# Mirrored odd blocks and one more unit of the products with B on GpSimd, in a stack of state-space scans

## The chip, the cores and the metric

The kernel runs on one core of a Trainium2 chip. The metric is the time of one execution in microseconds, as the device reports it; a kernel's time is the median of its runs. The engines are named as in the profile: PE (TensorE), ACT (ScalarE), DVE (VectorE), POOL (GpSimd) and SP (SyncE, which here issues the DMAs).

## The reference

Eight images of 48 x 48 positions and 96 channels pass through four residual layers. Layers 0 and 3 are 2-D selective scans (called "2-D" below, `ss2d` in the code), layer 2 scans every line of the image separately ("lines"), layer 1 is a spectral layer with no scan and is not touched. The core of a scan, cut to what matters:

```
xs = stack([x0, x1, x0[..., ::-1], x1[..., ::-1]])   # rows, columns, both reversed: 4 directions k
dts, Bs, Cs = split(x_dbl)                           # projections of xs: 16 states N each for B and C
delta = softplus(dts + bias)
def step(h, inp):                                    # over the positions of the sequence
    dA = exp(dl[..., None] * A)
    h  = h * dA + (dl * u)[..., None] * Bv[:, :, None, :]
    y  = einsum('bkdn,bkn->bkd', h, Cv)              # sum over the 16 states
    return h, y
```

Each direction has 192 channels with 16 states. In the 2-D layers one sequence covers the whole image (2304 positions), so a state goes on from row to row; in the lines layer every line of 48 positions starts from zero.

## The kernel before

**Blocks and turns.** A sequence of 2304 positions is cut into five blocks (`BLKS`, L25): four full ones of 10 rows (480 positions) and a short one of 8 rows (384), number 4. `scans` (from L172) walks over 8 images x 4 directions x 5 blocks = 160 blocks a layer, backwards through the blocks in the reverse directions. A block has 8 half-turns, or slots (`NG = 8`), each of a group of states and half of the channels. A slot holds three units; a unit is 128 partitions (32 channels x 4 states) by the positions of the block. Two slots make a turn, so a block has four turns q = 0 to 3, and a turn has six units in one `dbu` buffer, of which there are four.

**A turn, in the order of the code (L350 to L395).** ScalarE makes the decays `exp(dt * A)` in PSUM (`make_da`, L255), two units at a time, in two buffers. VectorE and GpSimd multiply `dt*u` by B (`make_dbu`, L235). In even slots VectorE makes all three units; in odd slots `ON_POOL` (L40) says how many of the three GpSimd makes. VectorE reads B from a copy in PSUM that ScalarE makes (`copy_b`, L216), GpSimd from the `bc` tile in SBUF. VectorE then scans two units in one instruction (`scan`, L263), in place in `dbu`, backwards for the reverse directions. GpSimd multiplies the states by C in place, three units at a time (`make_hc`, L276), and TensorE sums over the states (`reduce`, L296 and L298). In turn t the code works on the first products of turn t+1, and the products with C of the second half of turn t-1.

**Carried states.** One scan instruction runs over two units laid end to end. In the 2-D layers a unit therefore has one column more than positions (`columns`, L67: m = n + 1). Its decay is exp of a huge negative number, zero (`FAR`, written by the memset in `make_du`, L427), so the scan forgets what came before, and its addend is the state that the previous block left. The state travels in three steps. After a scan GpSimd copies the last column of three units into a small tile `carry` (`keep`, L270). One block later ScalarE copies six carried states (or `zero`, for the first block of a direction) into the extra columns of the new `dbu` (`bring`, L243), just before the decays of the next turn. The scan of that turn picks them up. In the lines layer no state is carried; the first position of each line has zero decay instead.

**Work beside the turns.** Two blocks ahead, `stage1` makes the inputs of a block step by step, one step at each half-turn, called from `aside`: projections on TensorE, softplus on ScalarE (L629, with its table loads), `dt*u` on GpSimd (`make_du`, L422), stores to DRAM (`store_dd`, L410), from where SP loads them broadcast over states (`load_dd`, L192, `load_bc`, L204). Convolutions, norms and the output of other images are strewn in the same way. Every engine takes its instructions in the order of the code.

Of the kernel before, what the change touches and what calls it, by code (L numbers as in the profile page):

```python
# [9 lines left out]
F32 = mybir.dt.float32  # L10
# [15 lines left out]
BMAX = 480  # L26
WMAX = BMAX + 1
NG = 8
# [10 lines left out]
CH = 96  # L39
ON_POOL = {1: 1, 3: 2, 5: 1, 7: 2}  # L40

# [17 lines left out]
class Block:  # L59


    def __init__(self, job, k, blk, first, last, rev):
        self.job, self.k, self.blk, self.first, self.last, self.rev = job, k, blk, first, last, rev
        self.r0, self.nr = BLKS[blk]
        self.n = self.nr * SEG

    def columns(self, restart):  # L67

        self.m = self.n + (0 if restart else 1)
        self.col = None if restart else self.n if self.rev else 0  # L70
        at = 0 if restart or self.rev else 1
        self.at = slice(at, at + self.n)


@with_exitstack
def vss_stack_kernel(ctx: ExitStack, tc: tile.TileContext, i: dict, out: bass.AP):
# [89 lines left out]
    def scans(dirs, order, restart, a, pools, ps, stage1, opening, done, side, tail):  # L166
# [6 lines left out]


        blocks = [Block(job, k, blk, n == 0, n == len(BLKS) - 1, dirs[k][1])
                  for job in range(nb) for k in order
# [4 lines left out]
        nt = len(turns)  # L181
        carry = pools["carry"].tile([P, 24], F32, tag="carry", name="carry")
        zero = pools["carry"].tile([P, 6], F32, tag="zero", name="zero")
        nc.gpsimd.memset(zero, 0.0)
        dbus, das, bps, bcs, ys = {}, {}, {}, {}, {}
# [9 lines left out]
        def load_bc(t):  # L195

            b, slot = blocks[t // NG], t % NG
            sg = ORDER[slot][1]
            other = t - slot + NG - 1 - slot
            n = min(free, key=lambda n: free[n])  # L200
            free[n] = other
            r = pools["bc"].tile([P, 2 * BMAX], F32, tag=f"bc{n}", name=f"bc{n}")
            rows4 = b.bcd[8 * sg:8 * sg + 8, :].rearrange("(s w) n -> s (w n)", w=2)
            nc.sync.dma_start(r[:, :2 * b.n], rows4.unsqueeze(0).to_broadcast([32, 4, 2 * b.n]))  # L204
            bcs[t] = bcs[other] = r[:, :2 * b.n].rearrange("p (w n) -> p w n", w=2)

        def copy_b(t):

            if t >= NG * len(blocks):
                return  # L210
            b, slot = blocks[t // NG], t % NG
            if slot == NG // 2:
                bps[t] = bps[t - 1]
                return
            bps[t] = ps("b", 1)
            nc.scalar.copy(bps[t][:, :b.n], bcs[t][:, 0, :b.n])  # L216

# [3 lines left out]
        def make_dbu(t, engine):  # L221

            if t >= NG * len(blocks):
                return
            b, slot = blocks[t // NG], t % NG
            if t // 2 not in dbus:
                dbus[t // 2] = pools["dbu"].tile([P, 6 * WMAX], F32, tag="dbu", name="dbu")
            cut = 3 - ON_POOL.get(slot, 0)
            lo, hi = (0, cut) if engine is nc.vector else (cut, 3)
            if lo == hi:  # L230
                return
            o = units(dbus[t // 2], b, 3 * (slot % 2) + lo, 3 * (slot % 2) + hi)[:, :, b.at]
            du = b.got[ORDER[slot][0]][:, lo:hi, 1, b.at]
            by = bps[t][:, :b.n] if engine is nc.vector else bcs[t][:, 0, :b.n]
            engine.tensor_mul(o, du, by.unsqueeze(1).to_broadcast([P, hi - lo, b.n]))  # L235

        def bring(t):

            if t >= nt or restart:
                return  # L240
            b, q = turns[t]
            o = units(dbus[t], b, 0, 6)[:, :, b.col]
            nc.scalar.copy(o, zero if b.first else carry[:, 6 * q:6 * q + 6])  # L243

# [12 lines left out]
        def scan(t, pair):  # L257
            b, q = turns[t]
            da = das.pop((t, pair))[:, :2 * b.m]
            db = dbus[t][:, 2 * pair * b.m:(2 * pair + 2) * b.m]  # L260
            if b.rev:
                da, db = da[:, ::-1], db[:, ::-1]
            nc.vector.tensor_tensor_scan(db, da, db, 0.0, ALU.mult, ALU.add)  # L263

        def keep(t, sub):
            b, q = turns[t]
            if b.last or restart:
                return
            last = b.at.start if b.rev else b.at.stop - 1
            nc.gpsimd.tensor_copy(carry[:, 6 * q + 3 * sub:6 * q + 3 * sub + 3], units(dbus[t], b, 3 * sub, 3 * sub + 3)[:, :, last])  # L270

        def make_hc(t, sub):
            b, q = turns[t]
            n = b.n
            h = units(dbus[t], b, 3 * sub, 3 * sub + 3)[:, :, b.at]
            nc.gpsimd.tensor_mul(h, h, bcs.pop(2 * t + sub)[:, 1, :n].unsqueeze(1).to_broadcast([P, 3, n]))  # L276

# [40 lines left out]
        for t in range(-2 * NG, 0):  # L318
            run(t)
        for half in range(2):  # L320
            load_dd(blocks[0], half)
# [6 lines left out]
        copy_b(2)  # L328
        bring(0)
        make_da(0, 0)  # L330
# [17 lines left out]
        for t, (b, q) in enumerate(turns):  # L348
# [7 lines left out]
            if t > 0:  # L356
                keep(t - 1, 1)
                make_hc(t - 1, 1)
# [11 lines left out]
            aside(at)  # L370
            bring(t + 1)
            keep(t, 0)
            make_hc(t, 0)
# [5 lines left out]
            if q == NG // 2 - 1 and b.k == order[-1] and b.last:  # L379
                for _ in beside:  # L380
                    while tail:
                        tail.pop(0)()
        keep(nt - 1, 1)
        make_hc(nt - 1, 1)
# [7 lines left out]
    def scan_pools(stack):  # L392
        def pool(name, bufs, **kw):
            return stack.enter_context(tc.tile_pool(name=name, bufs=bufs, **kw))
        ps = pool("ps", 1, space=PSUM)  # L395

        def psum(tag, bufs, n=512):
            return ps.tile([P, n], F32, tag=tag, name=f"ps_{tag}", bufs=bufs)

        pools = {"dd": pool("dd", 3), "bc": pool("bc", 1), "dbu": pool("dbu", 4),  # L400
                 "carry": pool("carry", 1), "dds": pool("dds", 1), "bcl": pool("bcl", 1),
                 "dr": pool("dr", 4, space=DRAM)}
        return pools, psum
# [13 lines left out]
    def make_du(b, half, u):  # L417
# [4 lines left out]
        nc.gpsimd.tensor_mul(rows(du, n), rows(dt, n), u)  # L422
        if b.col is None:
            at = SEG - 1 if b.rev else 0
            nc.gpsimd.memset(rows(dt, n)[:, :, at:at + 1], FAR)
        else:
            nc.gpsimd.memset(b.dds[:, half, :2 * b.m].rearrange("p (t m) -> p t m", t=2)[:, :, b.col:b.col + 1], FAR)  # L427


    def ss2d(l, xin, xout, b0=0):  # L430
# [163 lines left out]
        def stage1(b):  # L594
            n = b.n
            u = seq(us[b.job], dirs[b.k][0])[:, :, b.r0:b.r0 + b.nr, :]
            got = {}
# [42 lines left out]
        def so_far(b, half):  # L640
            if b.job not in yss:
                yss[b.job] = big.tile([DH, 2, L], F32, tag="big", name="ysum")
            return seq(yss[b.job][:, half], dirs[b.k][0])[:, b.r0:b.r0 + b.nr, :]

        def opening(b, half):

            if b.k == 0:
                return dskip[:, half, :], us[b.job][:, half, b.r0 * W:b.r0 * W + b.n]
            return wc["ident"], so_far(b, half)
# [480 lines left out]
```

## Time and profile before

| | |
|---|---|
| median of 3 runs | 19436.81 us (19431.89 to 19439.07) |
| the profiled execution | 19445.46 us, its span 19443.7 us |
| first to last scan, layer 0 / lines / layer 3 | 5807 / 6112 / 5810 us |
| busy: DVE, POOL, PE, ACT | 87%, 82%, 78%, 73% of the span |

A line of a group names the line of the kernel, the engine, the operation, what it writes and reads, and the shapes; then, after the count, its busy time in us, the mean ns of one instruction, and the idle time of the engine just before these instructions with what ended it. A line of a stretch gives the stretch, its length, and then the busy time (and number of instructions) of PE, PE's weight loads, DVE, ACT and POOL, and last the granted clock, the DMA engines' share and GB/s. A line of the order of time has a start, a length, and in brackets the idle time before it. A line of waits has who waited for whom, us in total, times, and the longest.

### The profile page before, as it was taken

Reading aid. Unit: us, or ns where it says so; the run is one execution under the profiler, and the core shown is the slowest. Engines: PE = TensorE matmul, PEld = TensorE weight load, DVE = VectorE, ACT = ScalarE, POOL = GpSimd, SP = SyncE. Lnnn points to the kernel's source line nnn. Section 1 sums busy time; section 2 is a strip of 40 time slices with the busy share of each in tenths; the row PEclk is TensorE's granted clock in tenths of the full one; section 3 lists DMA queues with packets and bytes.
Section 4 is the critical chain, followed back from the end, with each engine's and each line's share of the span. In section 5 each row is a group of like instructions: output and inputs, shape, how many; then the busy total and the mean of one; then the engine's idle time right before and its main releaser. Section 6 shows DMA issues by size and latency. Waiting matters only on the chain.

```text
span 19443.7 us, 172969 instructions
## 1 busy us (share of the span) xinstructions
PE 15206.3 (78%) x53500; PEld 4384.0 (23%) x53500; DVE 16830.2 (87%) x11289; ACT 14190.2 (73%) x22262; POOL 16019.2 (82%) x9825
## 2 busy tenths in 40 slices
PE   6777777777777897888888988887777777777776
PEld 1211211211114562222222222222121121121121
DVE  7999999999993228999999999997999999999998
ACT  6777877877872227788788787786778778778776
POOL 6999999999991007888888888886999999999998
PEclk6776776776767777888888878878677677677675
DMA  4444444444443324444434444443444444444444
GB/s 135 162 159 162 160 159 162 159 161 161 156 165 60 49 43 147 145 142 151 149 141 147 147 143 146 147 145 119 158 162 159 160 162 160 157 162 161 157 162 138
DMA packets 768487, 2829.45 MB, mean 146 GB/s; under 512 B 235724, under 2 KB 298668, under 8 KB 640926
## 3 DMA queue, kind: packets, MB, share of 16 engines
q1 hardware_dynamic: 767558, 2818.38, 44.1%
q8 instruction: 422, 6.91, 0.1%
q14 instruction: 507, 4.15, 0.1%
HBM read 2371.42 MB, written 446.69 MB: 145 GB/s over the span
## 4 chain that ended last, share of the span: by engine, by line
DVE 32%; PE 19%; POOL 16%; ACT 15%; issue 13%; DMA 5%; SPq 0%; POOLq 0%; DVEq 0%; ACTq 0%
DVE dbu L263 20%; POOL dbu L276 12%; DVE dbu L235 11%; ACT ps_da L255 4%; PE ps_s L740 3%; ACT L255 3%; PE ps_y L296 3%; DMA dd<-dd 2%; PE ps_h L970 2%; POOL dds L422 2%; PE ps_s L611 2%; PE ps_y L983 2%; PE ps_s L812 1%; POOL dbu L235 1%; PE ps_side L482 1%
## 5 line engine op out<-in xcount | busy, mean ns | idle before, releaser
L263 DVE TENSOR_TENSOR_SCAN dbu<-ps_da,dbu 128x962 f32<-128x962 f32 (+3 forms) x5760 | 11853.3, 2070 | 927.4 <-ACT ps_da L255 925.1
L276 POOL TENSOR_TENSOR dbu<-dbu,bc 128x1440 f32<-128x1440 f32 (+1 forms) x3840 | 11433.5, 2984 | 1051.2 <-DVE dbu L263 837.5
L255 ACT ACTIVATE ps_da<-dd,w_l_a 128x481 f32<-128x481 f32 (+3 forms) x11520 | 7414.9, 648 | 2754.7 <-DVE dbu L263 2548.7
L296 PE MATMUL ps_y<-dbu,w_red 128*32 128x480 f32 (+1 forms) x23040 | 4947.0, 747 | 2996.0 <-POOL dbu L276 2991.6
L298 PE MATMUL ps_y<-dbu,w_red 128*32 128x480 f32 (+1 forms) x7680 | 4906.1, 747 | 0.0
L235 DVE TENSOR_TENSOR dbu<-dd,ps_b 128x1440 f32<-128x1440 f32 (+5 forms) x3840 | 4641.3, 1209 | 261.3 <-ACT ps_b L216 217.7
L235 POOL TENSOR_TENSOR dbu<-dd,bc 128x480 f32<-128x480 f32 (+3 forms) x1920 | 3023.4, 1575 | 58.8 <-DMA bc<-bcd 35.5
L296 PEld LDWEIGHTS ps_y<-dbu,w_red 128*32 128x32 f32 x23040 | 743.6, 125 | 6938.7 <-POOL dbu L276 5185.4
L216 ACT COPY ps_b<-bc 128x480 f32<-128x480 f32 (+1 forms) x3360 | 1798.8, 535 | 298.9 <-DVE dbu L235 270.1
L740 PE MATMUL ps_s<-xpad,w_l_cw 128*128 128x480 f32 (+1 forms) x2560 | 1760.7, 840 | 2.3 <-ACT xpad L124 1.6
L482 PE MATMUL ps_side<-xpad,w_l_cw 128*128 128x480 f32 (+1 forms) x2880 | 1652.6, 703 | 4.5 <-ACT xpad L124 4.5
L255 ACT ACT_TABLE_LOAD x986 | 1265.0, 1283 | 17.5
L113 POOL MEMSET w_l_cw<- 128x1760 f32 (+1 forms) x3 | 5.8, 1941 | 1346.3 <-DVE x L950 1340.9
L422 POOL TENSOR_TENSOR dds<-dds,u 96x480 f32<-96x480 f32 (+1 forms) x640 | 791.9, 1237 | 202.9 <-ACT dds L629 202.9
L601 PE MATMUL ps_s<-bcl,dtw 6*96 6x480 f32 (+1 forms) x1280 | 880.6, 777 | 90.7 <-ACT dds L605 80.9
L611 PE MATMUL ps_s<-u,w_l_xp 96*38 96x480 f32 (+1 forms) x1280 | 931.7, 867 | 2.8 <-ACT dds L605 1.5
L270 POOL COPY carry<-dbu 128x3 f32<-128x3 f32 x2048 | 382.5, 187 | 635.0 <-DVE dbu L263 628.5
L292 PE MATMUL ps_y<-ysum,w_ident 96*96 96x480 f32 (+1 forms) x960 | 747.5, 868 | 114.1 <-ACT ysum L652 112.6
L482 PEld LDWEIGHTS ps_side<-xpad,w_l_cw 128*128 128x128 f32 x2880 | 581.1, 227 | 1130.4 <-issue 940.9
L740 PEld LDWEIGHTS ps_s<-xpad,w_l_cw 128*128 128x128 f32 x2560 | 531.8, 213 | 1096.4 <-issue 961.9
L298 PEld LDWEIGHTS ps_y<-dbu,w_red 128*32 128x32 f32 x7680 | 683.1, 125 | 0.0
L768 PE MATMUL ps_s<-bcl,dtw 6*96 6x480 f32 (+1 forms) x640 | 424.1, 799 | 181.7 <-ACT bcl L762 181.7
(146 smaller groups left out, 12660.7 us busy)
## 6 DMA issues: line engine op xcount, KB each, us to landing
dd<-dd SPq DMA_DIRECT2D x512, 1443.0 KB
bc<-bcd SPq DMA_DIRECT2D x1536, 480.0 KB
dd<-dd SPq DMA_DIRECT2D x256, 1440.0 KB
dd<-dds SPq DMA_DIRECT2D x512, 360.8 KB
dd<-dd SPq DMA_DIRECT2D x128, 1155.0 KB
bc<-bcd SPq DMA_DIRECT2D x384, 384.0 KB
dd<-dds SPq DMA_DIRECT2D x256, 360.0 KB
dd<-dd SPq DMA_DIRECT2D x64, 1152.0 KB
```

Source lines behind the costliest of these rows:

```text
L216: nc.scalar.copy(bps[t][:, :b.n], bcs[t][:, 0, :b.n])
L235: engine.tensor_mul(o, du, by.unsqueeze(1).to_broadcast([P, hi - lo, b.n]))
L255: nc.scalar.activation(da[:, at:at + b.m], b.got[half][:, u % 3, 0, :], AF.Exp, scale=a[:, b.k, ci:ci + 1])
L263: nc.vector.tensor_tensor_scan(db, da, db, 0.0, ALU.mult, ALU.add)
L276: nc.gpsimd.tensor_mul(h, h, bcs.pop(2 * t + sub)[:, 1, :n].unsqueeze(1).to_broadcast([P, 3, n]))
L296: nc.tensor.matmul(y[32 * g:32 * g + 32, :n], lhsT=wc["red"][:, :32], rhs=hc[:, g, b.at], start=False, stop=(slot == 3))
L298: nc.tensor.matmul(y[DH:, :n], lhsT=wc["red"][:, 32:], rhs=hc[:, 2, b.at], start=(slot == 0), stop=(slot == 3))
L422: nc.gpsimd.tensor_mul(rows(du, n), rows(dt, n), u)
L482: nc.tensor.matmul(pu[:, :n], lhsT=flat[:, at:at + P], rhs=xpad[:, r0 + dy:r0 + dy + nr, dx:dx + W], start=(tap == 0), stop=(tap == 8))
L601: nc.tensor.matmul(got["p"][:DH, :n], lhsT=dtw[2 * NS:, b.k, half, :], rhs=b.bcl[2 * NS:, :n], start=True, stop=True)
L611: nc.tensor.matmul(got["p"][:NBC, :n], lhsT=w[f"{l}_xp"][:, b.k, half, :], rhs=u[:, half], start=(half == 0), stop=(half == 1))
L740: nc.tensor.matmul(got["u", half][:, :n], lhsT=flat[:, at:at + P], rhs=shifted(off), start=(tap == 0), stop=(tap == 3))
```

## The change

**Mirrored blocks.** In the 2-D layers, blocks 1 and 3 are kept in reverse order of positions: `view` reads the inputs u, and reads and writes the sums y, backwards in both dimensions, and the scan of a mirrored block runs the other way through its buffer. A unit now has two columns more than positions (m = n + 2): one at the end where the scan begins (`came`), with decay zero as before, and one where it ends (`goes`), with decay 1 (dt = 0) and addend 0 (dt*u = 0), so that the scan leaves the final state there. The next block in the sequence scans in the opposite sense, and its `came` is the same column of the same buffer; the four buffers, `rooms`, are now allotted once, one to each turn of a block. So `keep`, `bring`, `carry` and `zero` are gone. `begin` has work only where a direction starts (a memset) and where the block's length changes between the short block and a full one (a copy of five states a partition on GpSimd).

**Where things lie.** The products with B take the column `goes` along, so that it becomes zero. The B and C rows in `bc` now start at element 1 of the tile instead of 0, in all three scan layers; `bc` tiles too are allotted once. `make_du` writes the end columns of both halves in two memsets, with the first half.

**The split.** In slot 5, in all three scan layers, GpSimd makes two of the three units instead of one.

```diff
-WMAX = BMAX + 1
+WMAX = BMAX + 2
-ON_POOL = {1: 1, 3: 2, 5: 1, 7: 2}
+ON_POOL = {1: 1, 3: 2, 5: 2, 7: 2}
...
     def columns(self, restart):
-        self.m = self.n + (0 if restart else 1)
-        self.col = None if restart else self.n if self.rev else 0
-        at = 0 if restart or self.rev else 1
-        self.at = slice(at, at + self.n)
+        self.mirrored = not restart and self.blk % 2 == 1
+        self.back = self.rev != self.mirrored
+        if restart:
+            self.m = self.n
+            self.at = self.by = slice(0, self.n)
+            return
+        self.m = self.n + 2
+        self.at = slice(1, self.n + 1)
+        self.came, self.goes = (self.m - 1, 0) if self.back else (0, self.m - 1)
+        self.by = slice(0, self.n + 1) if self.back else slice(1, self.n + 2)
+    def view(self, t, col):
+        v = seq(t, col)
+        if len(v.shape) == 3:
+            v = v[:, self.r0:self.r0 + self.nr, :]
+            return v[:, ::-1, ::-1] if self.mirrored else v
...
-            r = pools["bc"].tile([P, 2 * BMAX], F32, tag=f"bc{n}", name=f"bc{n}")
+            r = bufs[n]
-            nc.sync.dma_start(r[:, :2 * b.n], rows4.unsqueeze(0).to_broadcast([32, 4, 2 * b.n]))
-            bcs[t] = bcs[other] = r[:, :2 * b.n].rearrange("p (w n) -> p w n", w=2)
+            nc.sync.dma_start(r[:, 1:1 + 2 * b.n], rows4.unsqueeze(0).to_broadcast([32, 4, 2 * b.n]))
+            lead = b.at.start
+            bcs[t] = bcs[other] = r[:, 1 - lead:1 - lead + b.m], r[:, 1 + b.n:1 + 2 * b.n]
...
-        def bring(t):
+        def begin(t):
             if t >= nt or restart:
                 return
             b, q = turns[t]
-            o = units(dbus[t], b, 0, 6)[:, :, b.col]
-            nc.scalar.copy(o, zero if b.first else carry[:, 6 * q:6 * q + 6])
+            o = units(rooms[q], b, 0, 6)[:, :, b.came]
+            if b.first:
+                nc.gpsimd.memset(o, 0.0)
+            elif blocks[t // (NG // 2) - 1].m != b.m:
+                c = blocks[t // (NG // 2) - 1]
+                nc.gpsimd.tensor_copy(o[:, 1:], units(rooms[q], c, 1, 6)[:, :, c.goes])
...
-        def keep(t, sub):
-            b, q = turns[t]
-            if b.last or restart:
-                return
-            last = b.at.start if b.rev else b.at.stop - 1
-            nc.gpsimd.tensor_copy(carry[:, 6 * q + 3 * sub:6 * q + 3 * sub + 3], units(dbus[t], b, 3 * sub, 3 * sub + 3)[:, :, last])
...
             if t > 0:
-                keep(t - 1, 1)
                 make_hc(t - 1, 1)
...
-            bring(t + 1)
-            keep(t, 0)
+            begin(t + 2)
             make_hc(t, 0)
             make_da(t + 1, 0)
```

## The prediction

> **What bounds the kernel now.** I read the busy line and the groups of the page first, then one long stretch of each kind of layer, then groups by shape, then the order of time around the vector engine's stalls.
>
> ```profile
> PE 15206.3 (78%) x53500; PEld 4384.0 (23%) x53500; DVE 16830.2 (87%) x11289; ACT 14190.2 (73%) x22262; POOL 16019.2 (82%) x9825
> ...
> L263 DVE TENSOR_TENSOR_SCAN dbu<-ps_da,dbu 128x962 f32<-128x962 f32 (+3 forms) x5760 | 11853.3, 2070 | 927.4 <-ACT ps_da L255 925.1
> L276 POOL TENSOR_TENSOR dbu<-dbu,bc 128x1440 f32<-128x1440 f32 (+1 forms) x3840 | 11433.5, 2984 | 1051.2 <-DVE dbu L263 837.5
> ```
>
> See who waits for whom: idle time before the scans is ended by ScalarE's exponentials, 925.1 of 927.4 us, and never by GpSimd; GpSimd waits for the scans. By stretch (span, then PE, PEld, DVE, ACT, POOL), the first line 2-D (ss2d), the second lines:
>
> ```profile
> 2000.00:3000.00 1000.00, 761.78 (x2660) 197.05 (x2660) 934.04 (x591) 785.14 (x1272) 918.81 (x623) 0.74 0.48 161
> 9000.00:10000.00 1000.00, 834.86 (x2632) 222.82 (x2630) 923.63 (x629) 807.89 (x1172) 874.12 (x420) 0.81 0.41 144
> ```
>
> VectorE is the bound in both (934, 924), with GpSimd close behind (919, 874). From the scans taken in order, a 2-D block takes 36.3 us on average (5807 us over 160; a full one 37.4) and a lines block 38.2. Splitting the idle time before scans by its place in a full block: 2-D has 0.58 us before the first scan of a block (positive in 82% of full blocks) and 0.94 before the second; lines has 1.06 before the first scan of turn 0 and 0.67 before the first of turn 1. Turns 2 and 3 run without stalls in both.
>
> **Price of GpSimd's products.** Groups by shape, for a forward stretch of a 2-D layer (2310 to 2660 us), a reverse one (2680 to 3030), and lines (9000 to 9700):
>
> ```profile
> L276 POOL TENSOR_TENSOR dbu<-dbu,bc 128x1440 f32<-128x1440 f32 x60 | 179.2, 2986 | 4.8
> ...
> L235 POOL TENSOR_TENSOR dbu<-dd,bc 128x960 f32<-128x960 f32 x15 | 30.9, 2058 | 0.0
> ...
> L235 POOL TENSOR_TENSOR dbu<-dd,bc 128x480 f32<-128x480 f32 x14 | 14.5, 1036 | 0.0
> ```
> ```profile
> L276 POOL TENSOR_TENSOR dbu<-dbu,bc 128x1440 f32<-128x1440 f32 x67 | 205.4, 3068 | 10.5 <-DVE dbu L263 6.3
> ...
> L235 POOL TENSOR_TENSOR dbu<-dd,bc 128x480 f32<-128x480 f32 x18 | 21.4, 1189 | 0.0
> ```
> ```profile
> L276 POOL TENSOR_TENSOR dbu<-dbu,bc 128x1440 f32<-128x1440 f32 x115 | 371.3, 3244 | 59.7 <-DVE dbu L263 57.9 <-DMA bc<-bcd 1.7
> ...
> L235 POOL TENSOR_TENSOR dbu<-dd,bc 128x960 f32<-128x960 f32 x29 | 64.8, 2235 | 0.0
> L235 POOL TENSOR_TENSOR dbu<-dd,bc 128x480 f32<-128x480 f32 x28 | 34.0, 1213 | 3.1 <-DMA dd<-dd 3.1
> ```
>
> One shape has several prices. Lines gives a slow unit: 2235 - 1213 = 1.02 us; forward gives a fast one, 1036 - (1213 - 1022) = 0.85. Held against the columns where operands start, every row fits one rule: a unit is fast when its first operand starts 2 or 3 elements past a multiple of 4 relative to the second operand, slow at 0 or 1. Lines: all at 0, three slow. Forward half-turns: 1, 2, 3 (one slow, 2.90) and 0, 1, 2 (two slow, 3.07), mean 2.986; reverse: always two slow, 3.07. In all of these the second operand starts at a multiple of 4, so whether the difference or the first operand alone counts is not shown.
>
> **The change, part by part.**
>
> *The moved unit* (slot 5, every layer). VectorE's rows for two units and one are 1.129 and 0.629 in full blocks, 0.928 and 0.528 in short ones: -0.50 and -0.40 us a block. Against that, two more columns a scan: (2150 - 1750)/(962 - 770) = 2.08 ns an element, 12 scans, 0.050 us; one more column in 17 product units, 0.018. 2-D: 256 x 0.432 + 64 x 0.332 = 132 us. Lines (no wider rows): 128 x 0.50 + 32 x 0.40 = 77.
>
> A rule speaks against it. The Trainium skill, Perfetto Trace Analysis, section Optimizing Scalar/DVE Operations, says that moving work between VectorE and GpSimd may not help since they share an SBUF read port. By the rule the 132 would be 0 and the wider rows a loss of 21. The rows say otherwise: VectorE's one-unit product takes 628, 629 and 628 ns in the three stretches, scans 2149 to 2150, beside a busy GpSimd. I take the rows.
>
> *GpSimd's load.* The Trainium skill, GPSIMD Engine Reference, section Elementwise: about 2.6 cycles an element for two inputs, 1.04 us a unit at 1.2 GHz; the trace has 1.02 or 0.85. In 2-D the new columns (width 482, data from 1, C from 481) give two and one slow units alternately, mean 2.99 (before 3.03 over both directions), and make all products with B fast: 1.04 for one unit, 1.88 for two. Per full block: 8 x 2.99 + 1.04 + 3 x 1.88 = 30.6, against 8 x 3.03 + 2 x 1.12 + 2 x 2.06 = 30.6. The unit is free there. By the skill's price it is +1.0. The 2048 carry copies go (start to start 0.27 each, some 1.7 us a block); begin puts back 4 small instructions in two blocks of five, 0.4. The net is -1.3 us a 2-D block, or -0.3 by the skill. In lines B and C now start one past a multiple of 4 while data stay at 0: if the difference counts, all units are fast and GpSimd falls by some 4 us a block; if only the first operand counts, it rises by 1.0, from 874 to some 900 in 1000, still under VectorE.
>
> *ScalarE's carry copies go*, 1280 x 0.19 us, with their waits. In the order of time around the end of a block (ScalarE, then VectorE):
>
> ```profile
> 3120.62 1.28 ACT L629 ACT_TABLE_LOAD   x1
> 3121.91 0.85 ACT L629 ACTIVATE dds<-dds 96x768 f32<-96x768 f32 x1
> 3122.66 0.19 ACT L243 COPY dbu<-carry 128x6 f32<-128x6 f32 x1
> 3122.87 1.28 ACT L255 ACT_TABLE_LOAD   x1
> 3124.16 1.36 ACT L255 ACTIVATE ps_da<-dd,w_l_a 128x481 f32<-128x481 f32 x2
> ```
> ```profile
> 3125.56 2.16 DVE L263 TENSOR_TENSOR_SCAN dbu<-ps_da,dbu 128x962 f32<-128x962 f32 x1 [0.30 <-ACT ps_da L255]
> ```
>
> The copy stands between softplus and the exponentials that this scan waits for. Where that stall exists, 0.20 us of it go: the mean of min(stall, 0.20) is 0.16 in full and 0.15 in short blocks, 256 x 0.16 + 64 x 0.15 = 51 us. Next late is the exponential itself.
>
> *An earlier GpSimd in 2-D.* ScalarE's copy of the projections (L616) waits for a matmul queued behind reductions that wait for GpSimd, which sometimes stalls the second scan of turn 1 (0.11 us a full block, 1.38 a short one, 116 us in all). With 0.3 to 0.5 us less in front I take 25, ends 0 and 90.
>
> *Costed at nothing.* The 24 exponentials of a block grow by a column, 0.02 us in all at (664 - 582)/96 ns an element, under ScalarE's slack. begin sits on GpSimd before make_hc, and may wait there for the reductions of two turns ago; carry copies of like length went from the same place, and no VectorE wait ends with GpSimd. Its first reader is a turn later. Reversed reads of u, by matmul and make_du, and reversed writes of ysum: scans already run backwards at one price (2149, 2150); the upper end is the price of stride-48 columns, 1.44 for 1.03 to 1.20 (GpSimd) and 0.97 for 0.55 (ScalarE), in two blocks of five, covered by GpSimd's wait for scans and by ScalarE's slack in turn 2. If that cover fails, 0.2 us a block, 60 us. B and C land 4 bytes off: from nothing to a doubled packet time, on DMA engines 48% busy, for loads issued some four half-turns ahead. No DMA is moved; make_du's memsets stay two a block, and the store behind them on SP waits as before.
>
> *Where lines' 77 goes.* The faster product lies in turn 1, just ahead of a wait for another chain:
>
> ```profile
> DVE x L820 <- PE ps_s L812: 76.4, 74, 2.8
> ```
>
> The addition into x waits for a projection held up by ScalarE's silu of z in that turn, a chain started before the product. Counting L818 and L820 together, 109 of 160 blocks wait there, 0.72 us averaged over all 160. In those the 0.5 becomes wait; the other third keeps most of it: some 20 us of 77. Nothing stalls from there on until the next turn 0, so nothing is regained.
>
> **Sum.** 132 + 51 + 25 in 2-D, less some 15 that lands in other waits for TensorE, is 193; lines 20, and 25 more if GpSimd's faster rows bring its matmuls and loads forward. Together some 238 us of the profiled execution's 19445.5, which is 8.7 us above the median of the runs: 19,199 in the median's terms.
>
> **The rivals.**
> - As forecast, 19,110 to 19,290: chance 0.60.
> - Lines is freed too: fast units bring the projection forward, the 77 is kept, and a quarter microsecond a block each of waits for convolution matmuls and for dd goes: 19,437 - 193 - 77 - 80 = 19,087, down to 19,020. For: GpSimd's price. Against: silu of z, not GpSimd, ends that wait. 0.14.
> - The moved unit only lengthens ScalarE's and TensorE's waits in 2-D as well; the 51 and a little remain: 19,375. Against: turns 2 and 3 of 2-D have no such stall. 0.12.
> - Nothing within 0.2% (39 us, what can be told from no change here): gain and reversed reads cancel. 0.06.
> - Slower: GpSimd becomes the bound of 2-D. If the new starts make every unit slow, a full block costs it 8 x 3.25 + 1.21 + 3 x 2.24 + 2.9 of make_du + 0.3 = 37.1 us plus about 1 of unavoidable wait, 38.1 against the 37.4 of now: +0.7 x 307 full-block lengths (256 + 0.8 x 64) = 215 us, 19,650. It decides from 36.7 us on, the block that VectorE would need. Against: the rule fits every row. 0.08.
>
> Chances: faster 0.86, same 0.06, slower 0.08. The range, 19,040 to 19,375, leaves out the slow case, the null case and the tails, under 2 in 10.
>
> **What would show it.** Right: L243 and L270 gone; VectorE's two-unit products halved, from 960 instructions to 480; GpSimd's two-unit row near 1.88 in 2-D; the stall before a block's first scan down 0.2; 2-D layers near 5,710 us each, lines within 50 of 6,112. Wrong: scans idle behind GpSimd, GpSimd's 2-D products at 3.25, or VectorE's idle time in 2-D up by as much as its work went down.

## The result, and the profile after

The changed kernel takes 19144.19 us in the median of 4 runs (19128.96 to 19152.15), the kernel before 19435.77 on the same chip: a ratio of 0.985, 95% interval 0.9838 to 0.9862, so 292 us less. The forecast was 19,199. The profiled execution took 19152.15 us, its span 19150.3. From first to last scan:

| | before | after | forecast of the difference |
|---|---|---|---|
| layers 0 and 3 (2-D) together | 11616 | 11427 | -193 |
| lines | 6112 | 6018.5 | -20, or -45 with faster GpSimd rows |

The 2-D sum is right within 4 us, and its parts are not. Lines fell by 94, which is 48 or 73 more than the two forecasts. The page of the changed kernel, its busy line and two groups (L289 is the scan, L295 the products with C; L257, further below, the products with B):

```profile
PE 15031.5 (78%) x53500; PEld 4344.3 (23%) x53500; DVE 16643.8 (87%) x11289; ACT 14070.7 (73%) x20982; POOL 15110.6 (79%) x8304
...
L289 DVE TENSOR_TENSOR_SCAN dbu<-ps_da,dbu 128x964 f32<-128x964 f32 (+3 forms) x5760 | 11863.3, 2072 | 884.6 <-ACT ps_da L281 862.4
L295 POOL TENSOR_TENSOR dbu<-dbu,bc 128x1440 f32<-128x1440 f32 (+1 forms) x3840 | 10685.9, 2796 | 2290.8 <-DVE dbu L289 2202.6
```

VectorE works 186 us less (16830.2 before), and GpSimd 909 less although it makes one unit more; its idle time in front of the products with C has doubled (1051.2 before). The idle time of the scans fell by 43 only, and ScalarE still ends nearly all of it. VectorE's one-unit product has the length that it had (the kernel before, then the changed one):

```profile
L235 DVE TENSOR_TENSOR dbu<-dd,ps_b 128x480 f32<-128x480 f32 x768 | 482.6, 628 | 0.0
```
```profile
L257 DVE TENSOR_TENSOR dbu<-dd,ps_b 128x481 f32<-128x481 f32 x768 | 482.6, 628 | 0.0
```

The two stretches of before, in the changed kernel (columns as before: DVE is the third pair of busy time and count, POOL the fifth):

```profile
2000.00:3000.00 1000.00, 760.07 (x2683) 195.09 (x2682) 939.52 (x599) 786.54 (x1178) 901.95 (x497) 0.74 0.49 163
9000.00:10000.00 1000.00, 861.48 (x2636) 223.10 (x2635) 923.92 (x622) 815.86 (x1175) 789.08 (x421) 0.83 0.42 148
```

GpSimd falls by 17 in 2-D, and by 85 in lines (874 to 789). The DMA engines' share follows the bytes (0.41 at 144 GB/s before, 0.42 at 148 here, in lines): that B and C land 4 bytes off shows no cost. Why GpSimd fell is seen in its groups by shape, for a forward 2-D stretch (2280 to 2630 us) and for lines (9000 to 9700):

```profile
L295 POOL TENSOR_TENSOR dbu<-dbu,bc 128x1440 f32<-128x1440 f32 x60 | 178.6, 2990 | 31.0 <-DVE dbu L289 30.8
...
L257 POOL TENSOR_TENSOR dbu<-dd,bc 128x962 f32<-128x962 f32 x21 | 39.7, 1890 | 0.0
...
L257 POOL TENSOR_TENSOR dbu<-dd,bc 128x481 f32<-128x481 f32 x7 | 7.2, 1035 | 0.0
```
```profile
L295 POOL TENSOR_TENSOR dbu<-dbu,bc 128x1440 f32<-128x1440 f32 x127 | 346.0, 2734 | 116.5 <-DVE dbu L289 105.9 <-DMA bc<-bcd 10.6
L257 POOL TENSOR_TENSOR dbu<-dd,bc 128x960 f32<-128x960 f32 x47 | 88.5, 1884 | 0.0
```

In 2-D the rows are those of the prediction (2.99, 1.89 for 1.88, 1.04). In lines a product with C went from 3.24 to 2.73 us and one of two units from 2.24 to 1.88, though the data start where they did: B and C moved from element 0 to 1. So it is the difference of the start columns of the two operands that counts, which the prediction left open. A further reading is the wait that was to swallow the unit's gain in lines, that of the addition into x for a projection. In the waits of the changed kernel (before: 76.4 us):

```profile
DVE x L839 <- PE ps_s L831: 51.1, 54, 2.8
```

And in the order of time the copy of the carried states is gone from between softplus (L648) and the exponentials (L281) on ScalarE:

```profile
3077.55 1.28 ACT L648 ACT_TABLE_LOAD   x1
3078.85 0.85 ACT L648 ACTIVATE dds<-dds 96x768 f32<-96x768 f32 x1
3079.71 1.28 ACT L281 ACT_TABLE_LOAD   x1
3081.01 1.37 ACT L281 ACTIVATE ps_da<-dd,w_l_a 128x482 f32<-128x482 f32 x2
```

The stall in front of a block's first scan fell from 0.58 us to 0.47 in full blocks and from 0.95 to 0.65 in short ones: 47 us over the two layers, where the working had 51, but spread otherwise than by 0.2 a block.

### The profile page after: what moved, and what is told of

The parts are those of the page before. It is cut to its first block, busy times and chain, and to the rows that moved or that the text cites. A ratio compares the mean times of both kernels' runs of the same rounds, so it can differ in the third digit from the quotient of the medians.

```text
span 19150.3 us, 170303 instructions
## 1 busy us (share of the span) xinstructions
PE 15031.5 (78%) x53500; PEld 4344.3 (23%) x53500; DVE 16643.8 (87%) x11289; ACT 14070.7 (73%) x20982; POOL 15110.6 (79%) x8304
## 4 chain that ended last, share of the span: by engine, by line
DVE 26%; PE 22%; ACT 18%; issue 16%; POOL 13%; DMA 4%; SPq 0%; DVEq 0%; POOLq 0%; ACTq 0%
DVE dbu L289 15%; POOL dbu L295 10%; DVE dbu L257 10%; PE ps_s L759 5%; ACT ps_da L281 5%; ACT L281 4%; PE ps_y L315 3%; PE ps_h L989 2%; POOL dbu L257 2%; PE ps_side L501 2%; PE ps_y L1002 2%; PE ps_s L831 1%; PE ps_s L630 1%; DMA dd<-dd 1%; DMA dd<-dds 1%
## 5 line engine op out<-in xcount | busy, mean ns | idle before, releaser
L289 DVE TENSOR_TENSOR_SCAN dbu<-ps_da,dbu 128x964 f32<-128x964 f32 (+3 forms) x5760 | 11863.3, 2072 | 884.6 <-ACT ps_da L281 862.4
L295 POOL TENSOR_TENSOR dbu<-dbu,bc 128x1440 f32<-128x1440 f32 (+1 forms) x3840 | 10685.9, 2796 | 2290.8 <-DVE dbu L289 2202.6
L281 ACT ACTIVATE ps_da<-dd,w_l_a 128x482 f32<-128x482 f32 (+3 forms) x11520 | 7428.3, 648 | 2851.4 <-DVE dbu L289 2636.8
L257 DVE TENSOR_TENSOR dbu<-dd,ps_b 128x1443 f32<-128x1443 f32 (+10 forms) x3840 | 4414.3, 1150 | 264.6 <-ACT ps_b L238 217.0
L257 POOL TENSOR_TENSOR dbu<-dd,bc 128x962 f32<-128x962 f32 (+6 forms) x1920 | 3101.7, 1615 | 79.6 <-DMA dd<-dd 39.7
L238 ACT COPY ps_b<-bc 128x482 f32<-128x482 f32 (+3 forms) x3360 | 1805.0, 537 | 319.2 <-DVE dbu L257 288.5
L620 PE MATMUL ps_s<-bcl,dtw 6*96 6x480 f32 (+1 forms) x1280 | 837.9, 742 | 108.1 <-ACT dds L624 99.8
L776 PE MATMUL ps_s<-ub,w_l_xp 96*38 96x480 f32 (+1 forms) x640 | 382.7, 734 | 245.8 <-ACT ub L766 245.8
L800 PE MATMUL ps_s<-xpad,w_l_inz 96*96 96x480 f32 (+1 forms) x640 | 494.0, 904 | 97.6 <-ACT dds L794 80.9
```

The costliest lines, as they stand in the source:

```text
L238: nc.scalar.copy(bps[t][:, :b.m], bcs[t][0])
L281: nc.scalar.activation(da[:, at:at + b.m], b.got[half][:, u % 3, 0, :], AF.Exp, scale=a[:, b.k, ci:ci + 1])
L295: nc.gpsimd.tensor_mul(h, h, bcs.pop(2 * t + sub)[1].unsqueeze(1).to_broadcast([P, 3, n]))
L620: nc.tensor.matmul(got["p"][:DH, :n], lhsT=dtw[2 * NS:, b.k, half, :], rhs=b.bcl[2 * NS:, :n], start=True, stop=True)
```

## The experiments

Twelve kernels, each against the kernel before on the same chip. Spans are those of the profiled execution, from first to last scan; "short" is the busy time of VectorE's one-column operations in the group norms, on which more below. The medians of the kernel before, in the sets in which these ran, lie between 19425.88 and 19443.7, so a difference of under some 20 us between kernels of two sets is not told from none.

| kernel | us | ratio to before | 2-D | lines | short |
|---|---|---|---|---|---|
| before | 19435.77 | 1 | 11616 | 6112 | 94 |
| the change | 19144.19 | 0.985 (0.9838 to 0.9862) | 11427 | 6018.5 | 115 |
| unit only | 19361.73 | 0.9966 (0.9953 to 0.9978) | 11548 | 6100 | 100 |
| mirror only | 19241.98 | 0.9905 (0.9892 to 0.9919) | 11517 | 6018 | 81 |
| lines at 0 | 19240.65 | 0.9902 (0.9887 to 0.9918) | 11425 | 6122 | 96 |
| before, lines at 1 | 19351.52 | 0.996 (0.9947 to 0.9972) | 11618 | 6019 | 87 |
| ScalarE's copy back | 19155.15 | 0.9855 (0.984 to 0.987) | 11428 | 6015 | 84 |
| GpSimd's copies back | 19215.27 | 0.9889 (0.9873 to 0.9906) | 11492 | 6020 | 142 |
| B and C at 3 in 2-D | 19193.9 | 0.9876 (0.9861 to 0.9891) | 11474 | 6018 | 139 |
| slot 7 whole | 19030.02 | 0.9791 (0.9776 to 0.9806) | 11358 | 5984 | 154 |
| slots 5 and 7 whole | 18954.92 | 0.9756 (0.9743 to 0.9769) | 11353 | 5908 | 159 |
| the change, one-tensor norms | 19088.36 | 0.9825 (0.9812 to 0.9839) | 11375 | 6021 | 22 |
| mirror only, one-tensor norms | 19194.11 | 0.9878 (0.9865 to 0.9892) | 11482 | 6004 | 22 |
| slots 5 and 7 whole, one-tensor norms | 18856.34 | 0.9704 (0.9691 to 0.9717) | 11255 | 5892 | 22 |

**The unit alone**, in the kernel before.

```diff
-ON_POOL = {1: 1, 3: 2, 5: 1, 7: 2}
+ON_POOL = {1: 1, 3: 2, 5: 2, 7: 2}
```

> The kernel before with only the moved unit (slot 5: two units on GpSimd). Theory (the 2-D gain is VectorE's half microsecond, the lines gain needs GpSimd's faster rows): each 2-D layer loses some 75 us (from 5807 to about 5735), lines stays within 25 us of 6112, the whole about 19,270. Rival (the lines gain is the moved unit itself): lines falls by 75 us or more, the whole about 19,200. GpSimd's two-unit rows stay at 2.06 in 2-D and 2.23 in lines.

A third of a per cent. VectorE's products fell by 76 us a layer (here and below, without the stretch in which an instruction overlaps the next), but the 2-D layers by 31 and 37, half of what the theory had, and lines by 12. The scans' idle time grew; the page of this kernel (L263 is the scan), and its two groups of ScalarE's carry copies:

```profile
L263 DVE TENSOR_TENSOR_SCAN dbu<-ps_da,dbu 128x962 f32<-128x962 f32 (+3 forms) x5760 | 11852.0, 2069 | 991.9 <-ACT ps_da L255 985.1
```
```profile
L243 ACT COPY dbu<-carry 128x6 f32<-128x6 f32 x1024 | 196.6, 192 | 112.3 <-POOL dbu L235 67.1 <-DVE dbu L235 45.2
...
L243 ACT COPY dbu<-zero 128x6 f32<-128x6 f32 x256 | 50.0, 195 | 114.2 <-POOL dbu L235 63.2 <-DVE dbu L235 42.8 <-POOL carry L270 6.7
```

In the kernel before, the scans idled 927.4 us, and the copies' waits ended with GpSimd's products for 52.2 us against 130.3 here (the two lines together). But the copies' waits as a whole did not grow (239 us before, 226.5 here): only their last releaser changed. The wait of ScalarE that did grow stands in front of the step that adds the bias to dt (L605), which waits for TensorE's projection of dt (L601). In the waits of the kernel before and of this one:

```profile
ACT dds L605 <- PE ps_s L601: 51.6, 79, 2.0
```
```profile
ACT dds L605 <- PE ps_s L601: 123.2, 133, 2.0
```

In 2-D it grew from 41 to 112 us, nearly all of it in turn 3 of a block, and in 124 of 126 cases the projection stood on TensorE behind reductions that waited for GpSimd's products with C. In the 106 blocks in which this wait grew by over 0.15 us, the next block's first scan idles 41 us longer in all; in the other 212, 9 us less. So one more unit on GpSimd makes the scans late by way of TensorE and ScalarE.

**The mirroring alone**: the changed kernel with the old split.

```diff
-ON_POOL = {1: 1, 3: 2, 5: 2, 7: 2}
+ON_POOL = {1: 1, 3: 2, 5: 1, 7: 2}
```

> The changed kernel with slot 5 put back to one unit on GpSimd. Theory: each 2-D layer keeps only the copies' part, some 25 to 35 us (5775 to 5785 each); lines has the faster GpSimd rows without the moved unit and keeps 40 to 70 of its 93 us, so the whole is about 19,320. Rival (without the moved unit the faster rows are worth nothing in lines): lines at 6112 again, the whole about 19,380.

2-D is 99 us shorter than before, and lines, which has no carried states, already has its whole 94; both are more than the theory had. On top of this the unit brings 90 in 2-D and nothing in lines. Alone the unit brought 68 in 2-D. The two parts help each other by some 20 us there: beside the mirroring, the unit lengthens ScalarE's wait for the projection of dt from 16 to 32 us only, and the stalls in front of a block's first scan by 2 us, where it was 32 in the kernel before.

**Where B and C start, in lines.** First the changed kernel with the old start (the views of the tile move with it):

```diff
-            nc.sync.dma_start(r[:, 1:1 + 2 * b.n], rows4...)
+            base = 0 if restart else 1
+            nc.sync.dma_start(r[:, base:base + 2 * b.n], rows4...)
...
```

> The changed kernel, but in the lines layer B and C start at element 0 of their tile, as before (2-D untouched). Theory: GpSimd's products with C go back to 3.24 us in lines, TensorE's projection is late again, and lines gives back some 75 of its 93 us: about 6090, the whole about 19,220. Rival (the moved unit made the lines gain): lines stays near 6018 and the whole near 19,145, whatever GpSimd's rows cost.

Then the kernel before with the new start in lines alone (`base = 1 if restart else 0`, nothing else of the change):

> The kernel before, but in the lines layer B and C start at element 1 of their tile (2-D untouched, no moved unit). Theory: GpSimd's products with C fall from 3.24 to 2.73 us and with B from 1.21 and 2.23 to 1.04 and 1.88 there, the projection comes 0.6 us earlier and the wait of the addition in turn 1 nearly goes: lines at 6040 to 6070, the whole 19,365 to 19,395. Rival (GpSimd is hidden anyway): rows fall, lines stays within 10 us of 6112.

Four bytes are the whole gain in lines. Put back to 0, lines takes 6122; moved to 1 in the kernel before, 6019, without mirroring or unit; both moves are larger than their theories had. The wait for the projection follows, in the waits of the kernel with lines at 0 and of the kernel before with lines at 1:

```profile
DVE x L840 <- PE ps_s L832: 139.6, 95, 2.4
```
```profile
DVE x L821 <- PE ps_s L813: 18.8, 20, 2.8
```

The projection needs a PSUM buffer that silu of z, two instructions on ScalarE, sets free. In turn 1 of the 126 full blocks of lines that can be followed, the first of the two ends 6.26 us and the second 6.71 us after the turn's first scan starts, on average, both in the kernel before and in the changed one. The projection started at 6.69 before and at 6.32 after, and ended at 9.38 and 8.76. It started just when silu's first half ended in some 50 of the 126 blocks before, in some 120 after. In the others of before, 75 or so, it stood behind reductions that waited for GpSimd's products with C.

**ScalarE's copy put back.** The changed kernel, with a copy of 6 unused elements where the carry copy stood:

```diff
+            if t + 1 < nt and not restart:
+                nc.scalar.copy(sink, zero)
             begin(t + 2)
...
```

> The changed kernel, with a copy of 6 elements put on ScalarE in every turn of the 2-D layers at the place where the carry copy stood, from one unused tile to another, so that it waits for nothing. Theory (the copy cost time because it stands ahead of the exponentials that a block's first scan waits for): the stall before that scan grows back by some 0.15 us in 320 blocks, about +45 us, 19,190. Rival (the copy's own time was hidden, and what it cost was its wait for the product that GpSimd makes): +10 us or less.

11 us by the medians, and the intervals of the two kernels overlap: nothing that can be told from zero. The profile has a reason for caution. The scans' idle time did rise, by 23 us in 2-D (28 more in front of a block's first scan, 5 less elsewhere), but the short operations of the group norms took 31 less by another timing, and 2-D is as long as without the copy (11428, 11427). The theory's 45 is not there; that the copy costs nothing at all isn't shown either.

**GpSimd's copies put back.** The changed kernel with the 2048 small copies, into a tile that nobody reads (`keep` copies the last columns, as in the kernel before):

```diff
             if t > 0:
+                keep(t - 1, 1)
                 make_hc(t - 1, 1)
...
             begin(t + 2)
+            keep(t, 0)
             make_hc(t, 0)
...
```

> The changed kernel, with the 2048 carry copies put back on GpSimd (last columns of each half-turn to a tile that nobody reads), at their two places in every turn of the 2-D layers. Theory (GpSimd has room in 2-D, its copies hold up only the matmuls behind its products): GpSimd's busy time up by some 1.7 us a full block, time +10 to +30 us. Rival (GpSimd's queue carried the gain in 2-D): +50 us or more.

71 us, all of it in 2-D (65): the rival's side. The scans' idle time there rises by only 7. The rest is in short operations (27), in the normalisation of the sums behind TensorE's mean (17 more idle time in front of L541), and in small waits of products and other operations (13).

**GpSimd's products with B slower in 2-D.** The changed kernel with B and C starting at element 3 there:

```diff
-            nc.sync.dma_start(r[:, 1:1 + 2 * b.n], rows4...)
+            base = 1 if restart else 3
+            nc.sync.dma_start(r[:, base:base + 2 * b.n], rows4...)
...
```

> The changed kernel, with B and C starting at element 3 of their tile in the 2-D layers where the change has 1. By the rule of relative start columns GpSimd's products with B fall back to about 1.21 and 2.24 us, its products with C keep their mean. Theory (GpSimd is not the bound of 2-D): +1.2 us a full block on GpSimd, time 0 to +30 us, the 2-D layers within 10 us of 5,713. Rival (the speed of GpSimd's products carries the gain in 2-D as it does in lines): +80 us or more.

The groups by shape of its forward stretch give the predicted prices, and products with C stay:

```profile
L296 POOL TENSOR_TENSOR dbu<-dbu,bc 128x1440 f32<-128x1440 f32 x62 | 184.4, 2989 | 24.8 <-DVE dbu L290 24.3
L258 POOL TENSOR_TENSOR dbu<-dd,bc 128x962 f32<-128x962 f32 x22 | 49.4, 2243 | 0.0
...
L258 POOL TENSOR_TENSOR dbu<-dd,bc 128x481 f32<-128x481 f32 x7 | 8.5, 1214 | 0.0
```

The data stayed where they were, and B and C moved: the difference of the start columns counts here too. It cost 50 us, 48 of it in 2-D, between the two expectations. 1.2 us more a full block, on an engine with 98 us idle in 1000, is not free: again half of it (24) is in the short operations, 13 in front of L530, and 2 in front of the scans.

**All of slot 7 on GpSimd.** No copy of B by ScalarE is needed there then, and `copy_b` leaves it out (the last two lines).

```diff
-ON_POOL = {1: 1, 3: 2, 5: 2, 7: 2}
+ON_POOL = {1: 1, 3: 2, 5: 2, 7: 3}
...
+            if ON_POOL.get(slot) == 3:
+                return
```

> The changed kernel, with all three units of slot 7's product with B on GpSimd (two before), and ScalarE's copy of B for VectorE left out where nobody reads it. VectorE loses about 0.55 us a block in turn 2, where no stall stands behind it; GpSimd gains 0.85. Theory (VectorE is the bound, and a unit counts where no wait follows it): 2-D down by some 130 to 170 us in all, lines by 60 to 85, 18,900 to 18,950. Rival (GpSimd is now close enough to be late for VectorE in 2-D): lines gain, 2-D gives the gain back, 19,060 or more.

114 us less: about half of the theory in both kinds of layer (2-D -68, lines -35), and under the rival's bound. VectorE's products fell by 84 us a layer. Of the 168 in 2-D, 39 went into longer short operations and 35 into idle time of the scans.

**All of slots 5 and 7 on GpSimd**, in the same manner (`5: 3, 7: 3`).

> The changed kernel, with all three units of slots 5 and 7 on GpSimd (two and two before), and no copy of B for VectorE where nobody reads it. The run with slot 7 alone gave 19,030. Theory (in 2-D GpSimd nears the time of a block: about 34.7 of 35.5 us, so that a further unit is given back in waits behind it; in lines the wait for the projection in turn 1 takes it): 19,000 to 19,060, and the scans, or the short operations beside them, idle behind GpSimd. Rival (VectorE is still the only bound, a unit is worth its row): 18,900 to 18,950.

75 us less again, below what the theory allowed, and nearly all in lines (-76, against -5 in 2-D). For 2-D the theory was right: one more unit there comes back as waits, the scans' idle time alone growing by 108. ScalarE ends most of that, and the way is the one seen with the unit alone, in the waits of the kernel with slot 7 whole and of this one:

```profile
ACT dds L626 <- PE ps_s L622: 65.1, 91, 2.0
```
```profile
ACT dds L626 <- PE ps_s L622: 173.3, 182, 2.0
```

In lines the theory was wrong. With slot 5's copy of B gone, silu of z ends 5.98 us after the turn's first scan starts (6.71 before), and the projection at 8.05 (8.89 with slot 7 alone). Turn 1 falls by 0.87 us in full blocks, of which about half is left in the layer's time. The unit of the change, moved alone, was worth nothing in lines; this one, together with the copy that ScalarE is spared, is worth nearly VectorE's half microsecond a block. That it is the copy rests on these times: no run leaves out the copy alone. The two stretches of this kernel:

```profile
2000.00:3000.00 1000.00, 776.01 (x2705) 199.22 (x2704) 921.61 (x550) 756.50 (x1126) 951.08 (x499) 0.74 0.48 164
9000.00:10000.00 1000.00, 879.70 (x2694) 225.34 (x2687) 914.66 (x584) 800.01 (x1146) 848.59 (x434) 0.84 0.42 151
```

GpSimd is now the busiest engine of 2-D.

**The short operations.** In each group norm VectorE works out mean, square, sum and shift on one column. These instructions (L167, L168, L169, L179 of the changed kernel) have a length that depends on the kernel around them. Groups by shape of the changed kernel:

```profile
L179 DVE SCALAR_TENSOR_TENSOR shift<-gm,rs 96x1 f32<-96x1 f32 x32 | 57.8, 1807 | 1.1
...
L167 DVE TENSOR_TENSOR dev<-mv,gm 96x1 f32<-96x1 f32 x32 | 34.0, 1062 | 1.3
...
L169 DVE TENSOR_TENSOR dev<-dev,mv 96x1 f32<-96x1 f32 x32 | 13.1, 410 | 1.1
...
L168 DVE TENSOR_TENSOR dev<-dev 96x1 f32<-96x1 f32 x32 | 10.3, 322 | 1.1
```

An operation on one element a partition isn't work for 1.8 us. The order of time around one of them, VectorE and then GpSimd:

```profile
1147.41 0.13 DVE L177 RECIPROCAL rs<-rs 96x1 f32<-96x1 f32 x1
1147.58 4.28 DVE L179 SCALAR_TENSOR_TENSOR shift<-gm,rs 96x1 f32<-96x1 f32 x1
1151.78 2.15 DVE L289 TENSOR_TENSOR_SCAN dbu<-ps_da,dbu 128x964 f32<-128x964 f32 x1
```
```profile
1145.06 5.94 POOL L295 TENSOR_TENSOR dbu<-dbu,bc 128x1440 f32<-128x1440 f32 x2
1150.95 0.87 POOL L257 TENSOR_TENSOR dbu<-dd,bc 128x385 f32<-128x385 f32 x1
1151.76 0.20 POOL L269 COPY dbu<-dbu 128x5 f32<-128x5 f32 x1
```

It begins in the midst of a product with C on GpSimd (the first line has two), stands through the next, and ends at 1151.86 us with the third instruction, a product with B that ends at 1151.82. Of the 128 such instructions 46 take over 0.3 us, 102 us in all, and every one of them ends within 65 ns of the end of a GpSimd instruction (14 ns in the median); of the other 82, which take 0.16 us on average, 14 do. The experiment writes the same values with one tensor and a scalar of each partition:

```diff
-        nc.vector.tensor_sub(dev, mv[:, 0:1], gm)
-        nc.vector.tensor_mul(dev, dev, dev)
-        nc.vector.tensor_add(dev, dev, mv[:, 1:2])
+        nc.vector.tensor_scalar(dev, mv[:, 0:1], gm, None, op0=ALU.subtract)
+        nc.vector.tensor_scalar(dev, dev, dev, mv[:, 1:2], op0=ALU.mult, op1=ALU.add)
...
-        nc.vector.scalar_tensor_tensor(shift, gm, -1.0, rs, ALU.mult, ALU.mult)
+        nc.vector.tensor_scalar(shift, gm, rs, -1.0, op0=ALU.mult, op1=ALU.mult)
```

> The changed kernel, with the short operations on one column in the group norms (mean taken from mean, square, sum, shift) written as VectorE operations of one column with a scalar of each partition, so that none reads two tensors; values and engine are the same. In the changed kernel these 128 instructions take 115 us, and each of the 46 that take over 0.3 us ends within 65 ns of the end of a GpSimd instruction. Theory (a VectorE operation with two tensors in SBUF waits until GpSimd's instruction is over, and the profile shows that as busy): the 115 us fall to some 15, the time by 60 to 100, 19,045 to 19,085. Rival (the wait is for the operands, or a scalar's read waits in the same way): no change, 19,144 within 20.

Groups by shape of this kernel, the same work in 22 us:

```profile
L168 DVE TENSOR_SCALAR dev<-dev,mv 96x1 f32<-96x1 f32 x32 | 8.6, 269 | 1.2
...
L167 DVE TENSOR_SCALAR dev<-mv,gm 96x1 f32<-96x1 f32 x32 | 6.7, 209 | 1.3
L178 DVE TENSOR_SCALAR shift<-gm,rs 96x1 f32<-96x1 f32 x32 | 6.7, 209 | 1.1
```

The waits are gone, so it was the second tensor. Of the 93 us, 56 reach the time (51 in 2-D), a little less than the theory had; in lines the 20 saved there come back as other waits, of scans, products and additions.

**The unit again, without these waits**: the mirroring alone with one-tensor norms, to be held against the whole change with them. The edits are those above.

> The change without the moved unit (slot 5 with one unit on GpSimd, as before), with the short operations of the group norms written as operations of one tensor. With the run of the whole change in this form (19,088) it prices the moved unit where no short operation waits for GpSimd. Theory (with two-tensor operations the unit gained 91 us in 2-D, of 154 taken off VectorE, because 31 went into longer waits of these operations): the two runs differ by 110 to 130 us, 19,200 to 19,220. Rival (the waits of the short operations are an accident of timing, and the rest is given back elsewhere): they differ by 90 to 100, 19,180 to 19,190.

The two kernels differ by 106 us in their medians (106 in 2-D in the profiled executions), where with two-tensor norms the unit brought 98 (90 in 2-D). That falls between the two expectations; by the 2-D layers, 16 of the 31 us come back as time, and the rest turn into waits in front of the scans and for TensorE. But the four runs of this kernel alone lie 42 us apart, so the 16 is a hint and decides nothing.

**Both edits together**: slots 5 and 7 whole, and one-tensor norms, the version that the runs point to.

> The changed kernel with all three units of slots 5 and 7 on GpSimd, and the short operations of the group norms written as operations of one tensor. The first alone gave 18,955, with 159 us in the short operations; the second took 56 us of 93 off the changed kernel. Theory (the two add up): 18,870 to 18,900. Rival (in 2-D GpSimd is late by now, and what VectorE saves becomes waits for it): 18,930 to 18,955.

18856.34 us, 99 less than without the second edit and better than the sum expected. It beats both kernels: 0.9704 of before (0.9691 to 0.9717). Its page:

```profile
PE 15047.2 (80%) x53500; PEld 4304.2 (23%) x53500; DVE 16051.8 (85%) x10297; ACT 13546.3 (72%) x20022; POOL 15863.0 (84%) x8304
```

## Why the prediction was right, and where it was not

The bound was read rightly: VectorE in both kinds of layer, GpSimd with room. What was taken off VectorE and off its waits came through in part. By the steps of the working, in us for both 2-D layers together:

- **The moved unit, 132 after wider rows (153 before them).** Between the mirroring alone and the whole change VectorE's products fell by 154, as costed: their rows did not change (628 ns for one unit, beside a busier GpSimd). But 90 reached the time. The trace divides the 63 that came back: 31 in short operations that wait for GpSimd, 16 in front of the addition to the output (L572), 16 in front of the scans. The sum had allowed 15 for all such waits.
- **Wider rows, 21.** Between before and the mirroring alone, scans and products grew by 13 and 6.
- **ScalarE's copies, 51, and the earlier GpSimd, 25.** The scans' idle time fell by 72 with the mirroring, and where the working had it: 49 in front of a block's first scan, 17 in front of the second scan of turn 1. The attribution is in part unproven: a copy put back on ScalarE adds 23 to the idle time, not 51, and copies put back on GpSimd add 7. What remains, some 42, stays open. It may be the copies' waits for the products in their buffer (239 us of ScalarE's idle time before), which no run put back alone, or the two kinds of copies acting together.
- **What the sum did not have.** The mirroring also took 44 us off waits in front of VectorE's work on the output (L510 to L529, L553 to L572, L521 to L540), with the sign opposite to the 15 that the sum took off for TensorE. GpSimd's copies, costed only through the 25, are the larger part of what the mirroring brought: put back, they cost 65 us in 2-D, of the 121 that the mirroring is worth beside the moved unit. 17 of these 65 are waits in front of that work on the output.
- So the mirroring was worth 99 where the terms 51, 25 and -21 make 55, and the unit 90 where they leave 153. Less the 15 allowed for waits, two errors of 44 and 48 cancelled: that the 2-D total agreed within 4 us is luck.
- **Lines, 20 (45).** This is the mis-sized term of the total: 94. The rival "lines is freed too" was put aside because silu of z ends that wait. Silu held the projection in some 50 of 126 blocks; in most of the rest it stood behind reductions that waited for GpSimd. So the faster rows could bring the projection forward, as that rival had it. Its other half did not come: the 77 of the moved unit did vanish in lines, as the forecast argued (mirror only and the whole change: 6018 and 6018.5). What the forecast gave 25 us, GpSimd's faster rows, is the whole gain, and its sign of being right, lines within 50 of 6,112, did not come.
- **GpSimd's prices.** The rule for fast and slow units held in every row, and the start columns' difference is what counts. It also explains a loss that the working did not have: with the wider tile, `make_du`'s second half starts at column 964 instead of 962, and its product of a full block in rows went from 1.03 to 1.19 us, some 23 us of GpSimd in all. Reversed reads and writes cost nothing: `make_du` took 1194 ns forward and 1197 in mirrored blocks, the copy of the sums 547 in both.
- **The rule set aside.** I had put the Trainium skill's sentence on the shared read port (Perfetto Trace Analysis, Optimizing Scalar/DVE Operations) against VectorE's rows, and taken the rows. For the products that was right. The rule has a narrower form in the skill's SBUF — State Buffer, section Who interferes with whom: outside its two-port modes, a VectorE instruction contends with GpSimd's reads only if it has two inputs in SBUF. By the Summary of the same page, the one that comes second then blocks until the first has finished. The products read B from PSUM, the scans their decays; the one-column operations of the norms had both in SBUF, and show the block. The trace differs in one point: an operation stood through three GpSimd instructions, not only through the one that was there first. That is where the rule charged the moved unit: 31 us of 154, not all of it.

The slower rival, GpSimd as the bound of 2-D at 3.25 us a product, did not come. Its point of decision was not so sharp: GpSimd's work costs time well before it fills the block (1.2 us more a full block, on some 33 of 37, cost 48 us), through the short operations and the matmuls behind its products. The reading that no VectorE wait ends with GpSimd hid this: the wait ends with ScalarE or TensorE, and these had waited for GpSimd.

## What to carry to other kernels

Read an instruction's length against its size: an operation on one element a partition that took a microsecond or more was here a wait that the profile books as work, and each ended with an instruction of the engine that it had waited for. Before work is moved to an engine with room, ask which queues stand behind that engine's products (here reductions, then a projection, then a step of ScalarE), since these pay before the engine is full. When a forecast comes out right, test its terms one by one; here two of them were wrong by some 45 us each, in opposite senses.

## What the hardware showed that was not expected

- GpSimd's product of two fp32 tensors takes 0.85 or 1.02 us for a unit of 480 elements, by the difference of the operands' start columns modulo 4. Shifting one operand by 4 bytes took a product of three units from 3.24 to 2.73 us, and lines from 6112 to 6019.
- A VectorE operation with two tensors in SBUF, one element long in each partition, stood in the changed kernel up to 4.3 us through three GpSimd instructions in a row. The same with a scalar of each partition in place of the second tensor takes 0.21 us (0.27 with two scalars), and none of the 96 waited.
